# A two-layer graph network on one core: smaller last groups, and a block's inputs loaded a group early

## The chip, the cores and the metric

The kernel runs on one core of a Trainium2 chip. A core has TensorE (PE in the profile; its weight loads are PEld), VectorE (DVE), ScalarE (ACT), GpSimd (POOL) and SyncE (SP), each with its own queue of instructions that it takes in order, and 16 DMA engines. The metric is device time in microseconds (us) for one execution. The kernel before was timed three times: 4756.89, 4762.15 and 4760.23 us, median 4760.23.

## The reference, cut to what matters

There are 12,500 nodes of 128 numbers and 200,000 edges, sorted by destination. An edge's type is the argmax of ten of its 42 attributes. Each layer takes, for every node and type, the mean of the source rows of its edges, multiplies it by the matrix of the type and sums over types; a second matrix (root) is applied to the node's own row.

```python
def _rgcn_layer(x, src, dst, edge_type, w_rel, root, bias):
    N = x.shape[0]
    seg = dst * NUM_REL + edge_type
    xs = x[src]
    sums = jax.ops.segment_sum(xs, seg, num_segments=N * NUM_REL)
    cnt = jax.ops.segment_sum(jnp.ones(seg.shape, x.dtype), seg, num_segments=N * NUM_REL)
    mean = (sums / jnp.maximum(cnt, 1.0)[:, None]).reshape(N, NUM_REL, -1)
    return jnp.einsum('nrd,rdo->no', mean, w_rel) + x @ root + bias
...
edge_type = jnp.argmax(msg[:, NODE_EMB_DIM:-NODE_EMB_DIM], axis=1).astype(jnp.int32)
h = jax.nn.relu(_rgcn_layer(x, src, dst, edge_type, w_rel1, root1, b1))
return _rgcn_layer(h, src, dst, edge_type, w_rel2, root2, b2)
...
x = _layernorm(x + _L0_gnn_ref(...), axis=-1)
```

The second layer gathers rows of `h` from anywhere, so none of its gathers can start before the whole of `h` is written.

## The kernel before

**Tiles and groups.** The edges form 1563 tiles of 128, and the tiles form groups (`groups`, L67): 97 of 16 tiles, then one of 8 and one of 3. For each layer, `layer` (L518) goes over the groups.

**What a group does.** `sums` (L454) issues one gather for each tile on GpSimd (L445; tile `g`, a ring of three groups), lets VectorE build one-hot matrices `oh` (L461; two buffers) and placing matrices `at` (L465), and multiplies `g` by `oh` on TensorE into `zp` (L468): for each tile 12 neighbouring nodes by 10 types. ACT copies `zp` to `zs` (L482; four tiles an instruction). `project` (L487) multiplies `zs` by the ten type matrices, ten matmuls for each half of 8 tiles (L494), and ACT copies the result to `ms` (L500 or L498). `add` (L505) places the rows with `at` (L510) and VectorE adds them to the accumulators of all nodes, `acc` (L516), at an offset that it has loaded from `bt`. `b8` holds the first node of each tile of a group, from which `at` is made.

**Order in the loop.** In the turn of group k, the add of group k-2 is written first, then `sums` of k, then `project` of k-1. In an ordinary group the `zp` matmuls run from the last tile to the first, so that the first of them waits for all gathers of the group. In the last two turns (`end`, L536) they run forward, each after its own gather, and projection and addition of older groups are written earlier. The text is in program order; a scheduler then sets the order of each engine's queue, from the dependencies and its own estimates of time, within what the buffers allow. An engine takes its queue in order.

**Finishing a block.** Nodes are finished in blocks of 512 (23 of them), then of 128 (five) and 84, as soon as all edges that can reach a block are added (`done_after`, L76). `add_oldest` (L527) calls `block_in` (L373) and then `hidden` (layer 1) or `final` (layer 2). `block_in` has SP load the block's rows of x (`xb`; in layer 2 also its rows of h, `hb`; one buffer each), transposes them on TensorE (L386, up to four matmuls) into a PSUM tile `pf` and lets ACT copy that to `fT` (L388). `block_rows` (L391) adds the bias on VectorE (`a`, L395) and multiplies `fT` by the root matrix (L400) and `a` by the identity (L401), by turns, into another `pf`. `hidden` ends with a ReLU (L414) and a store to `hD`; `final` adds `xb` (`v`, L426), normalizes and stores the output. The two `pf` buffers also serve the counting of edges (`count`, L325), which runs beside layer 1 for the next 128 tiles at a time.

Of the kernel before, what the change touches and what calls it, by code (L numbers as in the profile page):

```python
# [20 lines left out]
P = 128  # L21
# [5 lines left out]
G = 16  # L27
QB = 4
HT = 8
# [5 lines left out]
CT = 128  # L35
YB = 512
W = 128
GT = 125
# [5 lines left out]
def rgcn_resnorm_kernel(ctx: ExitStack, tc: tile.TileContext, x, src, dst, attr, w_rel1, root1, b1,  # L44
# [14 lines left out]
    nc = tc.nc  # L59
    N, C = x.shape  # L60
    E = src.shape[0]
    D = attr.shape[1]
    CE = CT * P
    NT = -(-E // P)
    NCH = -(-NT // CT)

    groups = [(t, G) for t in range(0, NT - G + 1, G)]  # L67
    t = NT // G * G
    groups += [(t, HT), (t + HT, NT - t - HT)] if NT - t > HT else [(t, NT - t)]
    NG = len(groups)  # L70
    NPAD = N + SW
    starts = list(range(0, N - YB - 2 * P, YB))
# [1 line left out]
    NBLK = len(starts)  # L74

    def done_after(k):  # L76

        if k == NBLK - 1:
            return NT
        f = starts[k + 1] / N  # L80
        t = int((E * f + 5 * (E * f * (1 - f)) ** 0.5) / P) + 2
        if t >= NT:
            return NT
        return min(a + n for a, n in groups if a + n >= t)

    HALF = NT * P - E
    assert C == P and E % GT == 0 and 0 < HALF < P and NT % CT and groups[-1][1] > 1

    const = ctx.enter_context(tc.tile_pool(name="const", bufs=1))
    dram = ctx.enter_context(tc.tile_pool(name="dram", bufs=1, space=DRAM))  # L90
# [52 lines left out]
    def then(engine, ins):  # L143

        if engine in loaded:
            loaded.remove(engine)
            tc.keep_in_program_order(ins)
        return ins
# [74 lines left out]

    bt = keep.tile([1, NG], I32, name="bt")
    b8_i = keep.tile([G, NG], I32, name="b8_i")
    full = NT // G
    nc.vector.memset(b8_i[:, full:], 0)
    nc.scalar.dma_start(bt[:, :full + 1], bass.AP(dst.tensor, dst.offset, [[1, 1], [G * P, full + 1]]))
    nc.scalar.dma_start(b8_i[:, :full], bass.AP(dst.tensor, dst.offset, [[P, G], [G * P, full]]))
    for k, (t, n) in list(enumerate(groups))[full:]:  # L230
        if k > full:
            nc.scalar.dma_start(bt[:, k:k + 1], bass.AP(dst.tensor, dst.offset + t * P, [[1, 1], [1, 1]]))
        m = n if t + n < NT else n - 1
        nc.scalar.dma_start(b8_i[:m, k:k + 1], bass.AP(dst.tensor, dst.offset + t * P, [[P, m], [1, 1]]))
    nc.scalar.dma_start(b8_i[m:n, NG - 1:], bass.AP(dst.tensor, dst.offset + E - P, [[1, 1], [1, 1]]))
    b8 = keep.tile([G, NG], F32, name="b8")
    place = keep.tile([HR, 2, NG], F32, name="place")
# [119 lines left out]
    def block(k):  # L357
        n0 = starts[k]
        n = (starts + [N])[k + 1] - n0
        return n0, n, [(t, min(P, n - t * P)) for t in range(-(-n // P))]  # L360

    def rows_dma(sb, dr, k, store):
        n0, n, _ = block(k)
        full = n // P
        pairs = []
        if full:
            pairs.append((sb[:, :full], dr[n0:n0 + full * P, :].rearrange("(t p) c -> p t c", p=P)))
        if n % P:
            pairs.append((sb[:n % P, full], dr[n0 + full * P:n0 + n, :]))
        for a, b in pairs:  # L370
            then("SP", nc.sync.dma_start(b, a) if store else nc.sync.dma_start(a, b))

    def block_in(k, l):  # L373

        n0, n, subs = block(k)
        last = "e" if k == NBLK - 1 else ""
        b = len(subs) if last else 4
        xb = fin.tile([P, b, C], F32, name="xb" + last)
        rows_dma(xb, x, k, False)
        fb = xb  # L380
        if l:
            fb = fin.tile([P, b, C], F32, name="hb" + last)
            rows_dma(fb, hD, k, False)
        pt = ps_f.tile([P, YB], F32, name="pf")
        for t, h in subs:
            nc.tensor.transpose(pt[:, t * P:t * P + h], fb[:h, t, :], ident[:h, :h])  # L386
        fT = fin.tile([P, b * P], F32, name="fT" + last)
        nc.scalar.activation(fT[:, :n], pt[:, :n], AF.Copy)  # L388
        return xb, fT
# [53 lines left out]
    def gather(table, t0, n):  # L443
        g = gpool.tile([P, G, C], F32, name="g")
        return g, [then("POOL", nc.gpsimd.indirect_dma_start(  # L445
            out=g[:, j, :], out_offset=None, in_=table, in_offset=bass.IndirectOffsetOnAxis(
                ap=idxE[:, t0 + j:t0 + j + 1], axis=0))) for j in range(n)]
# [3 lines left out]
    def halves(n):  # L451
        return [(h, min(HT, n - h * HT)) for h in range(-(-n // HT))]

    def sums(table, k, end):  # L454

        t0, n = groups[k]
        g, gathers = gather(table, t0, n)
        oh = dpool.tile([P, G, KW], F32, name="oh")
        for j in range(n):
            t = t0 + j  # L460
            then("DVE", nc.vector.tensor_scalar(oh[:, j, :], iotaP[:, :KW], keyE[:, t:t + 1], wE[:, t:t + 1],  # L461
                                                op0=ALU.is_equal, op1=ALU.mult))
        at = spool.tile([HR, 2, SW], F32, name="at")
        for h, _ in halves(n):
            nc.vector.tensor_scalar(at[:, h, :], iotaP[:HR], place[:, h, k:k + 1], None, op0=ALU.is_equal)  # L465
        zp = ps_z.tile([P, G // QB, YB], F32, name="zp")
        for j in range(n) if end else reversed(range(n)):
            m = nc.tensor.matmul(zp[:, j // QB, j % QB * KW:(j % QB + 1) * KW], g[:, j, :], oh[:, j, :],  # L468
                                 start=True, stop=True)
            then("PE", m)  # L470
            if end:
                continue
            if j < n - 1:
                tc.keep_in_program_order(m)
                continue

            for d in gathers[:j]:
                tc.add_manual_dep(m.ins, d.ins.name, whole, reason="one wait per group")
        zs = zpool.tile([P, NREL, G, WN], F32, name="zs")
        for b in range(-(-n // QB)):  # L480
            m = min(QB, n - b * QB)
            then("ACT", nc.scalar.activation(  # L482
                zs[:, :, b * QB:b * QB + m, :],
                zp[:, b, :m * KW].rearrange("c (j r n) -> c r j n", r=NREL, n=WN), AF.Copy))
        return k, zs, at
# [32 lines left out]
    def layer(table, l, finish, steps, flag_too=False):  # L518

        done = 0  # L520
        held, projected = [], []
        ready = flag = None

        def project_oldest():
            projected.append(project(l, *held.pop(0)))

        def add_oldest():  # L527
            nonlocal done
            k, ms, at = projected.pop(0)
            add(k, ms, at)  # L530
            while done < NBLK and sum(groups[k]) >= done_after(done):
                finish(done, ready if done == NBLK - 1 else block_in(done, l))
                done += 1

        for k in range(NG):
            end = k >= NG - 2  # L536
            if projected:
                add_oldest()
            if end:

                if held:
                    project_oldest()
                if not ready:
                    ready = block_in(NBLK - 1, l)
                    if flag_too:
                        loads, (flag,) = nc.values_load_multi_w_load_instructions(
                            flag_i[0:1, 0:1], min_val=0, max_val=1, skip_runtime_bounds_check_because=HELD)
                        for ld in loads:
                            tc.keep_in_program_order(ld)
                        loaded.update(("POOL", "DVE", "PE", "ACT", "SP"))  # L550
            held.append(sums(table, k, end))
            if end and projected:
                add_oldest()
            if len(held) > 1:
                project_oldest()
            if steps:
                till, left, s = steps[0]
                for _ in range(max(1, -(-left[0] // max(1, till - k)))):
                    left[0] -= 1
                    if next(s, steps) is steps:  # L560
                        steps.pop(0)
                        break
        while held or projected:
            if held:
                project_oldest()
            if projected:
                add_oldest()
        return flag
# [13 lines left out]
    for a in range(0, NPAD, YB):  # L582
        m = min(NPAD - a, YB)
# [7 lines left out]
    for c in range(1, NCH):  # L591
        s = [as_steps(sources, c + 1), types(c + 1)] if c + 1 < NCH else []
        todo.append((c * CT // G - 1, [8 + L // DB + 2], chain(*s, count(c))))
    layer(x, 0, hidden, todo)
    def flagged():

# [14 lines left out]
        yield  # L611

    flag = layer(hD, 1, final, [(NG // 2, [1], flagged())], True)
    fast.close()

# [157 lines left out]
```

## Time and profile before

| | |
|---|---|
| median of three runs | 4760.23 us |
| profiled execution, its own time | 4772.34 us |
| its span, first to last instruction | 4770.4 us |
| mean granted TensorE clock | 0.739 |
| PE, PEld busy | 2759.5 us (58%), 2520.6 us (53%) |
| POOL busy | 2955.2 us (62%) |
| DVE, ACT busy | 1511.5 us (32%), 527.0 us (11%) |
| first and last gather of layer 1 start | 4.3 us, 2389.5 us |
| first and last gather of layer 2 start | 2422.2 us, 4731.4 us |

Durations come from the one profiled execution. A row of the timeline has the start (us from the span's start), the duration, engine, line, operation, what is written and read, how many were merged, and in brackets how long the engine was idle before it and what ended that. A row of the groups has the line, engine, operation, names, shape and count, then busy us and mean ns of one, then the idle time just before them and what ended most of it. A row of the waits has the waiting engine and line, what it waited for, us in total, times, and the longest. A row of the windows has the stretch, its length, the busy us (and instructions) of PE, PEld, DVE, ACT and POOL, the granted clock, the DMA engines' busy share and GB/s. "issue" is idle time that ended with nothing that the profile shows; "remote" is a wait whose releaser it does not tell. A matmul in 32-bit floats is two records.

### The profile page before, as it was taken

How to read it: one execution, taken by the hardware profiler on the slowest of the kernel's cores; microseconds unless marked ns; L12 is line 12 of the kernel's file. 1: busy time of each engine (PE TensorE's matmuls, PEld its weight loads, DVE VectorE, ACT ScalarE, POOL GpSimd, SP SyncE). 2: the span in 40 equal slices, each digit the busy share in tenths (PEclk: the TensorE clock that was granted, in tenths of full speed). 3: DMA queues.
4: the chain of work that ended last, by engine and by line, in shares of the span. 5: the costliest groups of instructions: out<-in, count | busy, mean ns of one | idle time of the engine just before them, and what ended most of it. 6: DMA issues, size and time to landing. Idle time of an engine off the chain costs nothing.

```text
span 4770.4 us, 43637 instructions
## 1 busy us (share of the span) xinstructions
PE 2759.5 (58%) x16162; PEld 2520.6 (53%) x16162; DVE 1511.5 (32%) x4652; ACT 527.0 (11%) x1136; POOL 2955.2 (62%) x3142
## 2 busy tenths in 40 slices
PE   2455556555655555666645555666655656565656
PEld 1455555555554545555544555555555555555556
DVE  5233333333333333333222222222222223222323
ACT  1011111111111101111110111111111111111111
POOL 5666665666656666666546666666666666666663
PEclk9677777777777777777776777777777777777778
DMA  4122122122221221212111211221222222222211
GB/s 141 44 79 74 50 74 74 50 75 62 61 77 47 75 62 51 57 48 52 46 49 46 54 52 51 53 56 51 52 56 53 52 52 58 51 52 52 58 52 40
DMA packets 180554, 279.00 MB, mean 58 GB/s; under 512 B 55623, under 2 KB 127190, under 8 KB 177206
## 3 DMA queue, kind: packets, MB, share of 16 engines
q0 software_dynamic: 100032, 205.07, 16.9%
q1 hardware_dynamic: 75428, 69.58, 4.6%
q8 instruction: 132, 2.16, 0.2%
q10 hardware_dynamic: 4872, 1.45, 0.1%
q14 instruction: 90, 0.74, 0.1%
HBM read 262.28 MB, written 13.60 MB: 58 GB/s over the span
## 4 chain that ended last, share of the span: by engine, by line
another core or an unknown queue 34%; PE 33%; issue 21%; DVE 11%; ACT 1%; DMA 0%; DVEq 0%; ACTq 0%; SPq 0%
PE pp L494 16%; PE zp L468 11%; DVE oh L461 7%; PE pp L510 2%; PE pf L401 1%; PE pf L400 1%; DVE at L465 1%; ACT zs L482 1%; DVE acc L516 1%; PE pf L343 0%; PE pf L345 0%; PE pf L386 0%; DVE o L436 0%; DVE st L429 0%
## 5 line engine op out<-in xcount | busy, mean ns | idle before, releaser
L445 POOL DMA_INDIRECT g<-in_x_dram,idxE x1563 | 1475.9, 944 | 911.2 <-issue 445.8
L445 POOL DMA_INDIRECT g<-hD,idxE x1563 | 1476.6, 945 | 865.3 <-issue 455.6
L494 PE MATMUL pp<-w,zs 128*96 128x128 f32 x7840 | 1358.2, 336 | 860.4 <-issue 722.1
L494 PEld LDWEIGHTS pp<-w,zs 128*96 128x96 f32 x7840 | 1232.0, 212 | 982.9 <-issue 834.6
L461 DVE TENSOR_SCALAR oh<-bank,keyE,wE 128x120 f32<-128x120 f32 x3126 | 1000.1, 400 | 644.6 <-remote 576.6
L468 PE MATMUL zp<-oh,g 128*128 128x120 f32 x6252 | 1033.5, 325 | 293.5 <-issue 259.9
L468 PEld LDWEIGHTS zp<-oh,g 128*128 128x128 f32 x6252 | 983.1, 240 | 314.0 <-issue 292.5
L482 ACT ACTIVATE zs<-zp 128x480 f32<-128x480 f32 (+1 forms) x782 | 382.9, 575 | 2167.7 <-remote 1912.9
L516 DVE TENSOR_TENSOR acc<-acc,pp 128x160 f32 x198 | 63.7, 322 | 1634.4 <-remote 1043.0
L510 PE MATMUL pp<-at,ms 96*128 96x160 f32 (+1 forms) x784 | 198.1, 386 | 591.1 <-issue 405.0
L510 PEld LDWEIGHTS pp<-at,ms 96*128 96x128 f32 (+1 forms) x784 | 142.5, 232 | 633.8 <-issue 437.1
L500 ACT ACTIVATE ms<-pp 96x256 f32<-96x256 f32 x196 | 74.1, 378 | 1241.3 <-remote 861.3
L341 DVE TENSOR_TENSOR eqb<-pf,kh 128x1344 bf16<-128x1344 f32 (+1 forms) x65 | 100.6, 1552 | 181.4 <-PE pf L345 82.3
L400 PE MATMUL pf<-root,fT 128*128 128x128 f32 x388 | 110.1, 379 | 79.0 <-issue 49.1
L401 PE MATMUL pf<-ident,a 128*128 128x128 f32 x392 | 114.0, 388 | 60.3 <-DVE a L395 22.0
L400 PEld LDWEIGHTS pf<-root,fT 128*128 128x128 f32 x388 | 87.0, 276 | 91.2 <-issue 55.8
L465 DVE TENSOR_SCALAR at<-bank,place 96x160 f32<-96x160 f32 x392 | 131.9, 376 | 0.0
L401 PEld LDWEIGHTS pf<-ident,a 128*128 128x128 f32 x392 | 90.7, 285 | 68.6 <-issue 24.6
L426 DVE TENSOR_TENSOR v<-pf,xb 128x512 f32<-128x512 f32 (+1 forms) x28 | 17.4, 620 | 243.2 <-remote 238.3
L348 DVE TENSOR_REDUCE wp<-pf 128x128 f32<-128x512 f32 (+1 forms) x13 | 9.0, 691 | 182.9 <-remote 175.5
L343 PE MATMUL pf<-eqb,identb 128*128 128x512 bf16 (+1 forms) x130 | 50.5, 388 | 17.9 <-DVE f L320 17.0
L388 ACT ACTIVATE fT<-pf 128x512 f32<-128x512 f32 (+1 forms) x56 | 30.2, 539 | 207.1 <-remote 151.3
(107 smaller groups left out, 483.0 us busy)
## 6 DMA issues: line engine op xcount, KB each, us to landing
m<-in_edge_attr_dram SPq DMA_DIRECT2D x24, 1344.0 KB
g<-in_x_dram,idxE POOLq DMA_INDIRECT x1563
g<-hD,idxE POOLq DMA_INDIRECT x1563
xb<-in_x_dram SPq DMA_DIRECT2D x46, 256.0 KB
hD<-hb SPq DMA_DIRECT2D x23, 256.0 KB
hb<-hD SPq DMA_DIRECT2D x23, 256.0 KB
out_dram<-o SPq DMA_DIRECT2D x23, 256.0 KB
w<-in_L_gnn_w_rel_dram ACTq DMA_DIRECT2D x2, 640.0 KB
```

Source lines behind the costliest of these rows:

```text
L341: nc.vector.tensor_tensor(eq[:p], kp[:p, None, :R].to_broadcast([p, DB, R]), ahead, op=ALU.is_equal)
L400: nc.tensor.matmul(pr[:h, t, :], fT[:, t * P:t * P + h], rsb[l], start=True, stop=False)
L401: nc.tensor.matmul(pr[:h, t, :], a[:, t * P:t * P + h], ident, start=False, stop=True)
L445: return g, [then("POOL", nc.gpsimd.indirect_dma_start(out=g[:, j, :], out_offset=None, in_=table, in_offset=bass.IndirectOffsetOnAxis(ap= ...
L461: then("DVE", nc.vector.tensor_scalar(oh[:, j, :], iotaP[:, :KW], keyE[:, t:t + 1], wE[:, t:t + 1], op0=ALU.is_equal, op1=ALU.mult))
L465: nc.vector.tensor_scalar(at[:, h, :], iotaP[:HR], place[:, h, k:k + 1], None, op0=ALU.is_equal)
L468: m = nc.tensor.matmul(zp[:, j // QB, j % QB * KW:(j % QB + 1) * KW], g[:, j, :], oh[:, j, :], start=True, stop=True)
L482: then("ACT", nc.scalar.activation(zs[:, :, b * QB:b * QB + m, :], zp[:, b, :m * KW].rearrange("c (j r n) -> c r j n", r=NREL, n=WN), AF.C ...
L494: nc.tensor.matmul(po[:m * WN, h], zs[:, r, h * HT:h * HT + m].rearrange("c j n -> c (j n)"), wsb[l][:, r, :], start=(r == 0), stop=(r == ...
L500: nc.scalar.activation(ms[:, :n // HT], po[:HR, :n // HT], AF.Copy)
L510: nc.tensor.matmul(pa, ms[:m * WN, h], at[:m * WN, h], start=(h == 0), stop=(h == len(parts) - 1))
L516: nc.vector.tensor_tensor(acc[:, s], acc[:, s], pa, op=ALU.add)
```

## The change

The groups are now 95 of 16 tiles, and the last 43 tiles form groups of 8, 8, 8, 8, 4, 4 and 3, so 102 groups in place of 99. `end` holds for these seven. In such a turn the adds and projections of older groups are all written first, `oh` and `at` of the next group (now made by `ones`) are written ahead of the projection, and the group is projected and added in its own turn. The ring stays at three groups. `bt` and `b8_i` are loaded with one pair of DMAs for each size of group: nine in place of six.

`block_in` of the next block to finish is written at the start of the turn after the one that finished the block before (from turn 1 on for the first), in place of right before the finish; the last block is excepted.

```diff
+    NS = NT // G - 2
+    groups = [(t, G) for t in range(0, NS * G, G)]
+    t = NS * G
+    while t < NT:
+        groups.append((t, min(HT if NT - t > 3 * QB else QB, NT - t)))
+        t += groups[-1][1]
...
-    def sums(table, k, end):
+    def ones(k):
         t0, n = groups[k]
-        g, gathers = gather(table, t0, n)
         oh = dpool.tile([P, G, KW], F32, name="oh")
...
+        return oh, at
+
+    def sums(table, k, oh, at):
+
+        t0, n = groups[k]
+        end = k >= NS
+        g, gathers = gather(table, t0, n)
...
             while done < NBLK and sum(groups[k]) >= done_after(done):
-                finish(done, ready if done == NBLK - 1 else block_in(done, l))
+                finish(done, ready if done == NBLK - 1 else given or block_in(done, l))
                 done += 1
+                given = None
         for k in range(NG):
-            end = k >= NG - 2
+            end = k >= NS
+            if k and not given and done < NBLK - 1:
+                given = block_in(done, l)
             if projected:
                 add_oldest()
             if end:
                 if held:
                     project_oldest()
+                    add_oldest()
...
-            held.append(sums(table, k, end))
-            if end and projected:
+            held.append(sums(table, k, *(made or ones(k))))
+            made = ones(k + 1) if end and k < NG - 1 else None
+            if end or len(held) > 1:
+                project_oldest()
+            if end:
                 add_oldest()
-            if len(held) > 1:
-                project_oldest()
```

## The prediction

> **What bounds the kernel now.** GpSimd issues all 3126 gathers, so I read its group on the page first, then its rows in the timeline.
>
> ```profile
> L445 POOL DMA_INDIRECT g<-hD,idxE x1563 | 1476.6, 945 | 865.3 <-issue 455.6
> L494 PE MATMUL pp<-w,zs 128*96 128x128 f32 x7840 | 1358.2, 336 | 860.4 <-issue 722.1
> ```
>
> 945 ns and a pipeline gap of 0.30 us make 1.25 us a gather, 20.0 us for a group of 16. The timeline of layer 2 shows what is added between groups:
>
> ```profile
> 2601.11 0.94 POOL L445 DMA_INDIRECT g<-hD,idxE  x1 [0.30 <-issue]
> 2605.60 0.94 POOL L445 DMA_INDIRECT g<-hD,idxE  x1 [3.54 <-remote]
> ...
> 2628.96 0.94 POOL L445 DMA_INDIRECT g<-hD,idxE  x1 [3.68 <-remote]
> ...
> 2792.63 0.94 POOL L445 DMA_INDIRECT g<-hD,idxE  x1 [3.57 <-remote]
> ...
> 2817.74 0.94 POOL L445 DMA_INDIRECT g<-hD,idxE  x1 [5.37 <-PE zp L468]
> ```
>
> A group's first gather waits for a buffer of the ring of three, so for the `zp` matmuls three groups back. Start to start an ordinary group takes 23.2 us: 20.0 of gathers and a pause of some 3.5 that hardly varies. PE's records cover about 13 of these 23.2, but they run ahead of what other engines see: results come late while gathers are in flight, and the last `zp` of a group is seen about 3.3 us after the last gather. I take the 23.2 as given. What varies is groups in which a block is finished. The 20 such groups in layer 2 from 2792 to 4616 take 24.1 to 25.7, mean 24.87: **1.67 us more** each.
>
> ```profile
> 2798.65 0.60 PE L386 MATMUL pf<-ident,hb 128*128 128x128 f32 x4
> ...
> 2801.95 0.60 ACT L388 ACTIVATE fT<-pf 128x512 f32<-128x512 f32 x1 [1.78 <-PE pp L510]
> ...
> 2805.53 0.32 DVE L516 TENSOR_TENSOR acc<-acc,pp 128x160 f32 x1 [8.39 <-remote]
> ...
> 2806.62 0.80 PE L401 MATMUL pf<-ident,a 128*128 128x128 f32 x2 [2.64 <-DVE acc L516]
> ```
>
> This is one of them. Transposes, their copy and the root matmuls (L400) stand in the same group, in PE's order, and PE stops for the copy. The waits give the sum (us, times, longest):
>
> ```profile
> PEld pf L400 <- ACT fT L388: 35.4, 12, 9.0
> ```
>
> **Block inputs a group early.** SP's loads, four transposes on PE and the copy on ACT move from the finishing group to the group after the previous finish, ahead of that group's add. Their number is unchanged. The trace has a sample: at the start of layer 2 the transposes of its first two blocks run at 2424 to 2429, long before the finishes in the groups that start at 2605.6 and 2698.7. These two groups take 23.4 and 24.3: 0.2 and 1.1 over 23.2, mean 0.65 against 1.67. So I take 1.0 us a finish, 20 finishes: **-20 us** in layer 2. In layer 1, 11 finishing groups with transposes in the same group average 25.3, 2.1 over: 1.45 each, **-16**. Of the others there most share their PSUM buffers with the counting of weights and end in counting groups of 28 to 30 us; I give them nothing. The sum, 36, is as large as the wait row above, though one is not derived from the other. Bounds: at best all the excess of layer 2 goes (24 finishes, 40 us) and the 2.1 of layer 1's eleven (23); at worst nothing.
>
> What the moved work costs: four transposes are 0.6 us of PE records in a group that is held at 23.2 anyway, and PE is then catching up after a finish; 46 times 0.15 = **+7**. Without that cover it is 46 x 0.6 = 28. On ACT the copy (0.60) comes behind `ms` and ahead of the next `zs`, which waits for PE until the group's end; nothing is late. On SP the order is the question: `xb` waits for `v` of the finished block (row at 2815.57, 22.9 into the group; the load goes out at 2816.29). If `hb` goes out behind it, 0.4 later, and lands in the 3.0 us that the load of 2421.32 took until PE's transposes at 2424.29, it is there 27 us after the finishing group's start, 2 into the next. PE gets to the transposes only behind `pp`, some 6 us in. Cover 4 us; if PE met them before, the `add` and all `zp` behind would stand for up to those 4 us.
>
> **The last 43 tiles.** Before, as 16, 16, 8, 3 (layer 1):
>
> ```profile
> 2368.72 0.94 POOL L445 DMA_INDIRECT g<-in_x_dram,idxE  x1 [4.88 <-PE zp L468]
> ...
> 2377.46 0.94 POOL L445 DMA_INDIRECT g<-in_x_dram,idxE  x1 [0.30 <-issue]
> 2387.03 0.94 POOL L445 DMA_INDIRECT g<-in_x_dram,idxE  x1 [8.63 <-PE zp L468]
> ...
> 2422.18 0.94 POOL L445 DMA_INDIRECT g<-hD,idxE  x1 [31.70 <-DMA hD<-hb]
> ```
>
> From 2321.0: 23.2 + 24.5 + 18.3 (8 tiles: 10 of gathers, 8.3 pause) + 3.5 + 31.7 = **101.2 us**. The 31.7 is a drain, and PE works in it:
>
> ```profile
> 2368.70:2387.00 18.30, 13.33 (x84) 13.14 (x84) 6.28 (x22) 2.83 (x8) 7.55 (x8) 0.74 0.20 51
> 2387.00:2422.20 35.20, 30.63 (x254) 28.33 (x252) 16.43 (x85) 9.29 (x26) 2.86 (x4) 1.00 0.11 30
> ```
>
> 30.6 of 35.2 us busy, at the full granted clock (1.00). So small groups remove little PE work: 7 groups need 70 `pp` matmuls where four need 60, one costs 0.21 us there, plus three adds: +3 us. And the ring holds three *groups*: smaller ones mean fewer tiles ahead. Step by step, each from one gather start to the next, PE bound (full speed: 16 `zp` 3.4, 20 `pp` 4.4, add and copies 1.5; 8 tiles: `zp` 1.7, wait for `zs` 1.2, `pp` 2.1, `ms` and add 1.1):
> - first 8: `pp`, add, 16 `zp` with 5 us lost beside 8 gathers, 15.5; second 8, with a block of 512, 19. Before, 23.2 and 24.5: -13.2.
> - third 8: two `pp` of 16, two adds with blocks, 8 `zp`: 21. Fourth 8: wait, `pp`, add, block, 8 `zp` with a loss: 12.
> - 4, 4: 7 each. The last 3: from its first gather, three groups of `zs`, `pp`, `ms`, add at some 5 (before, the 8 and the 3 took 4.7 and 5), the last block, store: 24.
>
> Sum 105.5, **+4 us a layer**. Bounds from the same rows: four groups of 8 at 13.3 (10 of gathers and the 3.3), two of 4 at 8.3 and 20 at the end give 90, -11; 18.3 for each 8, 10 for each 4 and 30 at the end, as before, give 123, +22. The sum lies between, and I keep it, since its steps are those of the rows just shown.
>
> **A rule against the row.** The Trainium skill, "TensorE: Matmul & The Clock Gate", section "HAM oscillation", says that PE's clock falls to half only after idle stretches of over about 3.4 us. My waits for `zs` are 1.2 us, so by the rule the end groups keep full speed. But the row of the one 8-tile group says 0.74: beside its gathers PE started nothing from 2374.9 to 2379.9, longer than its own waits would make it. By the rule my sum stays 105.5; by the row, for the fourth 8 and both 4s (3.8 us of `zp` and `pp` each: 11.4/0.74 - 11.4 = 4), it is 109.5. I take the row for the 8 alone, +1, and the rule for the 4s, whose 5 us of gathers are too short for such a stand: 106.5, **+5 a layer, +10 in all**.
>
> At the start three more small loads go out on ACT's queue (0.26 to 0.7 us each), ahead of the first activation at 16.3; the first `zp` is at 86. Nothing.
>
> **Sum**: -20 - 16 + 7 + 10 = **-19 us**. The profiled execution took 4772.34 (span 4770.4), 12 above the runs' median, so I take the 19 from the median 4760.23: **4741 us**.
>
> **Rivals.**
> 1. Both parts gain: early inputs give the 36 at no cost and the end 11 a layer: -58, 4702. For it: the drains, 32 and 38 us, are the largest single idle times of GpSimd. Against: PE is busy in them.
> 2. The small groups lose the prefetch: every group of 8 pays the pause of 8.3, every 4 one of 5: +22 a layer, -29 elsewhere: +15, 4775, slower. It decides once the seven groups take over 116 us (101.2 and half of the 29). For it: the 8.63 above. Against: that group had a whole 16 of `zp` behind it.
> 3. Transposes stand for `hb`: 4 us x 23 finishes in layer 2, +92 +10 and no gain, 4862. Against: the 4 us of cover.
> 4. The order on PE stays as it was, because the scheduler, not the program's text, places the transposes: only +10, 4770.
>
> **Chances**: forecast 0.42 (own range 4720 to 4756), rivals 0.20, 0.17, 0.08, 0.13. The range to hold 8 in 10 reaches to half of rival 1 and past rival 2: 4700 to 4786. With 0.2% (9.5 us) as what a measurement tells from no change: faster 0.53, same 0.16, slower 0.31.
>
> **What would show it.** Finishing groups of layer 2 at about 23.9 instead of 24.9, and the wait of L400 for `fT` near nothing; ordinary groups still 23.2. From the first gather of tile 1520 to layer 2's first gather 106, drain from the last gather below 25 instead of 31.7. It is wrong if ordinary groups grow, if transposes wait for DMA, or if the pauses after groups of 8 pass 8 us.

## Result and profile after

| | before | after |
|---|---|---|
| median, six runs each | 4757.30 us (4754.01 to 4762.15) | 4710.64 us (4699.18 to 4727.02) |
| profiled execution, its own time | 4772.34 us | 4727.02 us |
| its span | 4770.4 us | 4725.1 us |

The changed kernel takes 0.9908 of the time before (95% interval 0.9894 to 0.9922): 46.7 us less between the medians, 45.3 us between the two profiled spans. By the 0.2% that the prediction set as a limit that is faster, as forecast. It is inside the range to hold 8 in 10 (4700 to 4786), but the gain is more than twice the 19 us of the sum, outside the forecast's own range (4720 to 4756), and nearer to rival 1 (4702) than to the forecast (4741).

The spans are split at the first gathers of five stages. The first gather of tile 1520 starts the last 43 tiles.

| stage | before | after | difference | predicted |
|---|---|---|---|---|
| start, to the fourth group of layer 1 | 92.7 | 94.1 | +1.4 | 0 |
| layer 1, from there to tile 1520 | 2228.3 | 2200.7 | -27.6 | -16 + 3.5 |
| layer 1, last 43 tiles to layer 2's first gather | 101.2 | 98.2 | -3.0 | +5 |
| layer 2, to tile 1520 | 2240.5 | 2224.5 | -16.0 | -20 + 3.5 |
| layer 2, last 43 tiles to the end | 107.7 | 107.6 | -0.2 | +5 |

(The 7 us for moved transposes are shared out evenly.) Layer 2 came as worked out. Layer 1 gave twice as much, and the tails nothing worth the name. On the page of the changed kernel the rows of the gathers and of the projection are (busy us, mean ns, idle before):

```profile
L450 POOL DMA_INDIRECT g<-hD,idxE x1563 | 1476.8, 945 | 849.0 <-issue 452.7
L505 PE MATMUL pp<-w,zs 128*96 128x128 f32 x7880 | 1330.2, 333 | 675.3 <-issue 544.7
```

Neither engine works faster; both stand less. The timeline of layer 2 shows a finishing group and the group behind it:

```profile
2763.92 0.94 POOL L450 DMA_INDIRECT g<-hD,idxE  x1 [3.49 <-remote]
...
2769.49 0.39 PE L405 MATMUL pf<-root,fT 128*128 128x128 f32 x2
...
2777.85 0.80 PE L406 MATMUL pf<-ident,a 128*128 128x128 f32 x2 [3.98 <-DVE acc L527]
...
2787.49 0.94 POOL L450 DMA_INDIRECT g<-hD,idxE  x1 [3.88 <-PE zp L479]
...
2792.66 0.60 PE L391 MATMUL pf<-ident,hb 128*128 128x128 f32 x4
...
2803.16 0.38 ACT L511 ACTIVATE ms<-pp 96x256 f32<-96x256 f32 x1 [12.83 <-remote]
...
2803.59 1.44 PE L521 MATMUL pp<-at,ms 96*128 96x160 f32 x4 [10.32 <-issue]
...
2808.78 0.36 SPq L376 DMA_DIRECT2D hb<-hD  x1
2808.79 0.60 ACT L393 ACTIVATE fT<-pf 128x512 f32<-128x512 f32 x1 [5.25 <-remote]
...
2811.35 0.94 POOL L450 DMA_INDIRECT g<-hD,idxE  x1 [4.21 <-PE zp L479]
```

The finishing group (2763.92 to 2787.49, 23.6 us) begins its root matmuls with an `fT` that was made groups ago. The transposes of the next block (2792.66) stand one group later, and that group takes 23.9. Over the 22 finishing groups of layer 2 ahead of tile 1520 the mean is 23.71 (before 24.78); the groups behind them take 23.75 (before 23.36). The copy to `fT` comes at 2808.79, 15.5 us after the end of the transposes, and now nothing waits for it. ACT had the copy `ms` to do first, and that too starts 10.3 us after the end of its matmuls (2792.83); then ACT stands another 5.25 us. At the same moment SP's load goes out into the `hb` that the transposes read (2808.78, SPq). So two engines see PE's result that late. Whether the matmuls end later than they are drawn, or the news of it travels late, these rows don't tell.

The tail of layer 1, GpSimd's first gathers of its groups and of layer 2:

```profile
2306.74 0.94 POOL L450 DMA_INDIRECT g<-in_x_dram,idxE  x1 [2.29 <-PE zp L479]
...
2324.88 0.94 POOL L450 DMA_INDIRECT g<-in_x_dram,idxE  x1 [8.47 <-PE zp L479]
...
2344.65 0.94 POOL L450 DMA_INDIRECT g<-in_x_dram,idxE  x1 [10.08 <-PE zp L479]
...
2393.00 0.94 POOL L450 DMA_INDIRECT g<-hD,idxE  x1 [18.56 <-issue]
```

The drain fell from 31.7 to 18.6 us, and the pauses ahead of it took most of that back: 8.5 and 10.1 where there had been 4.9 and 8.6, and the last four groups start later by their own small pauses.

### The profile page after: what moved, and what is told of

The parts are those of the page before. It is cut to its first block, busy times and chain, and to the rows that moved or that the text cites. A ratio compares the mean times of both kernels' runs of the same rounds, so it can differ in the third digit from the quotient of the medians.

```text
span 4725.1 us, 43784 instructions
## 1 busy us (share of the span) xinstructions
PE 2749.6 (58%) x16206; PEld 2523.4 (53%) x16206; DVE 1509.7 (32%) x4660; ACT 529.7 (11%) x1142; POOL 2955.3 (63%) x3142
## 4 chain that ended last, share of the span: by engine, by line
another core or an unknown queue 37%; PE 29%; issue 18%; DVE 14%; ACT 1%; DMA 0%; DVEq 0%; ACTq 0%; SPq 0%
PE pp L505 13%; PE zp L479 10%; DVE oh L465 9%; PE pp L521 2%; PE pf L406 1%; PE pf L405 1%; DVE at L469 1%; DVE acc L527 1%; ACT zs L493 1%; PE pf L350 0%; PE pf L348 0%; PE pf L391 0%; DVE st L434 0%; DVE bank L275 0%
## 5 line engine op out<-in xcount | busy, mean ns | idle before, releaser
L505 PE MATMUL pp<-w,zs 128*96 128x128 f32 x7880 | 1330.2, 333 | 675.3 <-issue 544.7
L505 PEld LDWEIGHTS pp<-w,zs 128*96 128x96 f32 x7880 | 1218.7, 210 | 787.8 <-issue 649.8
L521 PE MATMUL pp<-at,ms 96*128 96x160 f32 (+1 forms) x788 | 206.5, 396 | 682.5 <-issue 498.5
L511 ACT ACTIVATE ms<-pp 96x256 f32<-96x256 f32 (+1 forms) x198 | 74.2, 375 | 1321.1 <-remote 1010.0
```

The costliest lines, as they stand in the source:

```text
L505: nc.tensor.matmul(po[:m * WN, h], zs[:, r, h * HT:h * HT + m].rearrange("c j n -> c (j n)"), wsb[l][:, r, :], start=(r == 0), stop=(r == ...
L511: nc.scalar.activation(ms[:, :n // HT], po[:HR, :n // HT], AF.Copy)
L521: nc.tensor.matmul(pa, ms[:m * WN, h], at[:m * WN, h], start=(h == 0), stop=(h == len(parts) - 1))
```

## Experiments

All ran beside the kernel before on the same chip, but on three chips: here A, B and C. The kernel before takes 3973 us on A, 4680 to 4686 us on B and C, against 4757 us in the first measurement ("the first chip" below). What follows is always a comparison on one chip.

Two things are followed throughout. One is the row of PE's weight loads for the root matmuls, with the time for which PE stood idle ahead of them. The other, matched block by block in the trace, is the lag from the end of a block's transposes to the start of the copy `fT`, over the 23 blocks of 512 in layer 1.

**1. One part alone (chip A).** The early inputs alone are this edit of the kernel before:

```diff
-                finish(done, ready if done == NBLK - 1 else block_in(done, l))
+                finish(done, ready if done == NBLK - 1 else given or block_in(done, l))
                 done += 1
+                given = None
...
+            if k and not given and done < NBLK - 1:
+                given = block_in(done, l)
```

> The kernel before with one part of the change: a block's inputs are loaded and transposed a group early; groups as before (97 of 16, 8, 3). Theory A, the early inputs are the gain: about 43 us below the kernel before (ratio 0.991), layer 2 from its first gather to that of tile 1520 about 16 us shorter, layer 1's some 28, and both tails as before (101 and 108 us). Theory B, the small last groups give a good part of it: at most 25 us below the kernel before.

The small groups alone are the rest of the change (`groups`, `bt`, `ones`, the order under `end`), with `block_in` left at the finish.

> The other part alone: the small last groups and their order in the loop, a block's inputs loaded where they are finished. Theory A: 0 to 4 us below the kernel before, tails of 98 and 107 us. Theory B: 15 us or more below. The recorded sum had this part at 10 us above.

Loads alone: `block_in` is cut in two, and only its loads go out early.

```diff
+            if k and not given and done < NBLK - 1:
+                given = block_in(done, l)
...
-        pt = ps_f.tile([P, YB], F32, name="pf")
+        return xb, fb
+
+    def turned(k, given):
...
+        pt = ps_f.tile([P, YB], F32, name="pf")
...
-                finish(done, ready if done == NBLK - 1 else block_in(done, l))
+                finish(done, ready if done == NBLK - 1 else turned(done, given or block_in(done, l)))
```

> The kernel before, with the loads of xb and hb alone written a group early; transposes, their copy and PE's queue stay as before. Theory A, PE's order is what counts (transposes, copy and root matmuls no longer in one group): within 5 us of the kernel before. Theory C, what the finish waited for was the loads: about 40 us below.

Transposes three times, where they stand before:

```diff
-        for t, h in subs:
+        for t, h in 3 * subs:
             nc.tensor.transpose(pt[:, t * P:t * P + h], fb[:h, t, :], ident[:h, :h])
```

> The kernel before, with every transpose of a block written three times where it is finished: 8 more a finish, 1.2 us of PE. Theory A, PE is late in a finishing group and pays for each instruction there: finishing groups of layer 2 grow by about 1.2 us, the whole by 45 to 55 us. Theory D, only the wait for ACT's copy counted: below 10 us.

Measured: kernel before 3972.95; early inputs 3972.90 (ratio 1.0000, 0.9991 to 1.0009); groups 3960.34 (0.9968, 0.9956 to 0.9980); loads 3973.74 (1.0002); three times 3973.40 (1.0000). Theory A's numbers failed in three of the four. Theory B's 15 us for the groups was missed too, by 2.4; theory D's number held. The run with the loads can't tell the theories apart here, since there was nothing to gain. The page of the run with early inputs says why:

```profile
L445 POOL DMA_INDIRECT g<-hD,idxE x1563 | 1475.3, 944 | 496.3 <-issue 462.0
...
L494 PE MATMUL pp<-w,zs 128*96 128x128 f32 x7840 | 892.9, 273 | 6.4 <-ACT zs L482 3.3
```

A gather still takes 944 ns, but GpSimd's idle time is 496 us in place of 865: nearly all of it the 0.30 us between two gathers. Ordinary groups take 20.0 us, with no pause. The projection's matmuls take 273 ns with 6.4 us of idle time, where the first chip showed 336 ns and 860 us in the kernel before. PE is ahead of the gathers, so nothing that it does in a finishing group is on the path, 8 more transposes included. The copy follows the transposes at once:

```profile
2785.35 0.60 PE L386 MATMUL pf<-ident,hb 128*128 128x128 f32 x4
...
2785.99 0.60 ACT L388 ACTIVATE fT<-pf 128x512 f32<-128x512 f32 x1
```

What is left on this chip is the drain between the layers, here with the groups of before and then with the small ones:

```profile
1992.70 0.94 POOL L445 DMA_INDIRECT g<-hD,idxE  x1 [20.26 <-DMA hD<-hb]
```

```profile
1983.64 0.94 POOL L450 DMA_INDIRECT g<-hD,idxE  x1 [12.07 <-issue]
```

8.2 us less, and from the last gather to the end 27.3 against 23.2: together 12.3, nearly the whole 12.6 of the measurement. Where PE isn't late the prediction's two parts change places.

**2. The changed kernel, and PE made late by force (chip B).** First the changed kernel as it is:

> The changed kernel itself, on the chip of this call. Where the kernel before takes some 3973 us here and GpSimd's gathers never pause (period of an ordinary group 20.0): all of the gain is that of the small last groups, 12 to 13 us below the kernel before. Where the kernel before takes some 4757 us (period 23.2): 40 to 48 us below, as first measured.

4634.64 against 4685.97, ratio 0.9896 (0.9881 to 0.9911): 51 us, a little above the 40 to 48. Its ordinary groups take 23.0 us: this chip resembles the first. Then the projection four times, without and with early inputs:

```diff
-            for r in range(NREL):
+            for r in 4 * list(range(NREL)):
                 nc.tensor.matmul(po[:m * WN, h], zs[:, r, h * HT:h * HT + m].rearrange("c j n -> c (j n)"),
                                  wsb[l][:, r, :], start=(r == 0), stop=(r == NREL - 1))
```

> The kernel before with every matmul of the projection run four times (each repeat starts its sum anew, so the result stays), some 13 us more of PE a group, so that PE is late wherever it runs. Theory A: ordinary groups grow to 23 us or more, finishing groups are longer still by 2 to 4 us; 4500 us or more in all. It is the base for the run that follows.

> The kernel above (projection four times) with a block's inputs loaded and transposed a group early, groups as before. Theory A, where PE is late it stops for the copy fT in a finishing group, and an early block takes that stop away: 0.5 to 1.5 us a finish for 46 finishes, 20 to 70 us below the kernel with the fourfold projection. Theory E, PE only carries the same instructions in another place and what was gained came from something else: within 5 us of it.

7406.44 and 7409.75 us: no gain (ratios 1.5808 and 1.5824, intervals of 0.0021 to either side). Theory A fails in the form given, "where PE is late it stops for the copy". PE is late here: an ordinary group takes 36.8 us, 13.8 over 23.0, which is 0.23 for each of its 60 added matmuls. Yet it hardly stops. In the first of the two the groups of instructions show 2.6 us of idle time (behind the bar) ahead of all root matmuls:

```profile
L400 PEld LDWEIGHTS pf<-root,fT 128*128 128x128 f32 x388 | 59.2, 192 | 2.6 <-ACT fT L388 2.5
```

The lag from transposes to copy is 0.04 us in all 23 blocks. In these groups the gathers stop 17 us before the group ends. Theory E's number (within 5 us) held, but with no stop to take away this pair can't speak for it; part 4 can. So PE being late isn't the condition; it is that its result is *seen* late, which on this chip went with gathers in flight, though not every time (part 4).

**3. The root matmuls early too (chip B).** In layer 2 the root matmuls of `fT` run in `block_in`, and `block_rows` adds only `a`:

```diff
+        if not l or k == NBLK - 1:
+            return xb, fT
+        pr = ps_f.tile([P, 4, C], F32, name="pf")
+        for t, h in subs:
+            nc.tensor.matmul(pr[:h, t, :], fT[:, t * P:t * P + h], rsb[l], start=(t == 0), stop=False)
+        return xb, pr
...
+        if l and k < NBLK - 1:
...
+            for t, h in subs:
+                nc.tensor.matmul(fT[:h, t, :], a[:, t * P:t * P + h], ident, start=False, stop=(t == len(subs) - 1))
+            return fT
```

> The changed kernel, in whose second layer the root matmuls of fT also run a group early, their sums held open in PSUM until those of a close them. Where PE is late (23.2 us a group): 5 to 15 us below the changed kernel, since the finishing groups' rest of 0.45 us over an ordinary one is PE work too. Where gathers never pause: within 3 us of the changed kernel.

4649.64 us: 15.0 *above* the changed kernel (ratio to before 0.9925 against 0.9896). Layer 2 as far as tile 1520 is 12.7 us longer; 10.3 of that is left when the one odd group of each kernel is taken out (9.5 and 6.7 us over the median, with no cause in the profile). Finishing groups are down to 23.08 (medians; 23.14 in the changed kernel), but the groups behind them take 23.67 in place of 23.07. There transposes and root matmuls stand in one group again:

```profile
3006.26 0.60 PE L391 MATMUL pf<-ident,hb 128*128 128x128 f32 x4
...
3013.01 0.60 ACT L393 ACTIVATE fT<-pf 128x512 f32<-128x512 f32 x1 [3.87 <-remote]
...
3013.66 2.08 PE L398 MATMUL pf<-root,fT 128*128 128x128 f32 x8 [2.72 <-issue]
...
3025.06 0.94 POOL L461 DMA_INDIRECT g<-hD,idxE  x1 [4.48 <-PE zp L490]
```

The copy starts 6.2 us after the transposes' end, PE stands until 3013.66, 0.05 us after the copy's end, and the next group's gathers start after a pause of 4.48 instead of 3.3. The groups of instructions have 49.8 us of idle time ahead of layer 2's root matmuls, where the changed kernel has 2.4:

```profile
L398 PEld LDWEIGHTS pf<-root,fT 128*128 128x128 f32 x194 | 41.5, 313 | 49.8 <-issue 26.6 <-ACT fT L393 23.2
```

So it isn't an early place that helps. A group *between* the transposes and the first reader of `fT` does, and this kernel took it away again.

**4. One part alone once more (chip B).** The edits of part 1.

> The early inputs alone once more (groups as before), for a chip on which PE is late. Where the kernel before takes some 4690 to 4760 us: theory A, the early inputs are nearly all of the gain, 35 to 50 us below the kernel before, finishing groups of layer 2 within 0.6 us of ordinary ones; theory B, the small last groups share it: 15 to 30 us below. Where it takes some 3973 us: no difference again.

> The small last groups alone once more. Where the kernel before takes some 4690 to 4760 us: theory A, within 8 us of the kernel before; theory B, 15 to 30 us below; the recorded sum, 10 us above. Where it takes some 3973 us: 12 to 13 us below again.

> The loads alone a group early, transposes, copy and PE's queue as before, once more. Where the kernel before takes some 4690 to 4760 us: theory A (PE's stop for the copy fT inside the finishing group was the cost), within 8 us of the kernel before; theory C (the loads were late), the same gain as with the transposes moved too. Where it takes some 3973 us: no difference again.

| chip B | median us | ratio (interval) | lag in layer 1: median, longest |
|---|---|---|---|
| before | 4684.03 | | |
| early inputs alone | 4636.21 | 0.9894 (0.9879 to 0.9909) | 3.10, 8.91 |
| small groups alone | 4684.56 | 0.9995 (0.9986 to 1.0005) | 2.91, 13.55 |
| loads alone | 4687.82 | 1.0004 (0.9995 to 1.0013) | 2.25, 13.12 |

Theory A holds here on all three counts, and B and C fall. All of the 48 us is that of the early inputs; loads without transposes bring none of it, groups bring none. The medians hide a split. With small groups or loads alone, ten of the 23 lags, all in groups with counting, are 10.6 to 13.6 us; their transposes end 9 to 13 us after the group's first gather. With early inputs the transposes stand elsewhere, and ten lags are 0.04 us: six with transposes in the first 3.6 us of a group, beside its gathers, and four behind a group's last gather. The other lags are 2.5 to 8.9 us, and PE no longer stands for them. The groups of instructions of the root's weight loads, with early inputs, with small groups, with loads alone:

```profile
L400 PEld LDWEIGHTS pf<-root,fT 128*128 128x128 f32 x388 | 69.7, 220 | 43.8 <-issue 39.8 <-DVE eqb L341 3.1 <-ACT fT L388 0.7
```

```profile
L405 PEld LDWEIGHTS pf<-root,fT 128*128 128x128 f32 x388 | 82.6, 263 | 137.5 <-ACT fT L393 77.5 <-issue 59.8
```

```profile
L408 PEld LDWEIGHTS pf<-root,fT 128*128 128x128 f32 x388 | 80.2, 255 | 136.0 <-ACT fT L396 80.4 <-issue 55.5
```

Not every "issue" is free of the copy: with loads alone, the first root matmul starts within 0.2 us of the end of its copy in 44 of the 46 blocks of 512. Counted by these starts, 134.7 of the 136.0 us are stops for the copy; with early inputs 1.1 of the 43.8 are. The stop is gone, but PE's standing mostly moved: ahead of the matmuls of `a` it rose from 28.8 to 110.1 us, so the two rows together lost 11 us while the kernel lost 48. What the change is worth can't be read from idle time; the lengths of the groups, below, tell it.

The two runs also show the wait at work. With loads alone, a finishing block in layer 1 beside the counting of edges:

```profile
719.58 0.66 PE L394 MATMUL pf<-ident,xb 128*128 128x128 f32 x4
...
724.76 0.51 PE L502 MATMUL pp<-w,zs 128*96 128x128 f32 x1 [1.14 <-issue]
...
731.96 0.38 SPq L371 DMA_DIRECT2D xb<-in_x_dram  x1
731.96 0.60 ACT L396 ACTIVATE fT<-pf 128x512 f32<-128x512 f32 x1 [17.06 <-remote]
...
732.27 0.94 POOL L453 DMA_INDIRECT g<-in_x_dram,idxE  x1 [3.43 <-remote]
...
732.61 0.80 PE L408 MATMUL pf<-root,fT 128*128 128x128 f32 x2 [7.34 <-ACT fT L396]
```

The transposes end at 720.24. ACT is idle (17.06 us) and starts the copy only at 731.96, when the group's gathers have stopped; SP's next load into `xb` goes out in the same moment. PE stands 7.34 us for the copy. The counting comes behind, and the next group takes 27.9 us. With early inputs, in the groups of the same tiles:

```profile
725.24 0.90 PE L386 MATMUL pf<-ident,xb 128*128 128x128 f32 x4
...
726.17 0.60 ACT L388 ACTIVATE fT<-pf 128x512 f32<-128x512 f32 x1 [0.99 <-PE pf L386]
```

By then the block before has its root matmuls behind it, these transposes belong to the next one, and the group takes 23.7.

Where it goes, from the traces of these two runs on one chip, each layer from its fourth group to tile 1520: layer 1, 2178.2 to 2144.3 (-33.9); layer 2, 2139.5 to 2130.3 (-9.2); the tails -3.5 and -3.8. In layer 1 the excess over the median group (23.04 and 23.06) fell from 35.6 to 12.0 us in the 36 groups with counting, and from 18.8 to 6.0 in the 12 finishing groups without it. In the groups with counting, two things changed at once: PE's stop went, and the blocks' two `pf` buffers, which the counting shares, are taken at another time. No run separates these.

**5. A deeper ring (chip C).** The changed kernel with `RING = 4` for `RING = 3`.

> The changed kernel with four group buffers for the gathered rows in place of three. It asks what holds an ordinary group at 23.2 us. Theory A, PE's rate beside gathers does, and a gather's pause only passes that on: where the kernel before takes 4690 to 4760 us, ordinary groups stay at 23 us and the whole within 10 us of the changed kernel (ratio to the kernel before 0.988 to 0.992). Theory F, the gathers wait only because the ring is short: the pauses of 3 us go, some 190 of them, 500 us or more below. Where the kernel before takes some 3973 us there are no pauses, and it equals the changed kernel (ratio 0.997).

4640.85 against 4679.65, ratio 0.9918 (0.9903 to 0.9932): not better than three buffers (0.9896 on chip B). Theory A holds. Two first gathers in layer 2:

```profile
2497.24 0.95 POOL L450 DMA_INDIRECT g<-hD,idxE  x1 [3.27 <-remote]
...
2520.27 0.95 POOL L450 DMA_INDIRECT g<-hD,idxE  x1 [3.32 <-remote]
```

The first pause comes a group later than with three buffers (after the fourth group of a layer), and then the period is 23.0 again. On chip B no run beat the changed kernel by more than the intervals leave open; on chip A it was not run.

## Why the prediction was right, and where not

**Early inputs, layer 2: right.** "So I take 1.0 us a finish": 1.07 (24.78 to 23.71). So close a hit is partly luck, since the sample was two groups, 0.2 and 1.1 us over. The moved work, put at 0.15 a group, cost 0.39 in the group behind (23.36 to 23.75) on the first chip and nothing on chip B. The net, -16.0, is within a microsecond of the -16.5; on chip B it was -9.2.

**Early inputs, layer 1: the mis-sized term.** "Of the others there most share their PSUM buffers with the counting of weights [...]; I give them nothing." On the first chip the excess over the median group (23.24 us before, 23.23 after) fell by 17.1 us (58.2 to 41.1) in the 36 groups with counting, on chip B by 23.6. That is the step that failed: a term put at nothing was worth the most, and even the bound "at best" for layer 1 (23) was passed by the 27.6. The finishing groups without counting gave 8.2 on the first chip (27.6 to 19.4), less than the 16, because one of them grew to 29.9; the other ten that had been long fell by 13.3. The block at 719.58 above is one of those with counting: there the lag is long, and so is the stop.

The warning was in the profile of before. The 35.4 us of waits for `fT` were set beside the sum of both layers ("as large as the wait row above") without asking where they lie. Here are the waits of these loads in layer 1, then those in layer 2 (us in total, times, longest):

```profile
PEld pf L400 <- ACT fT L388: 34.7, 11, 9.0
PEld pf L400 <- issue: 25.1, 13, 8.4
```

```profile
PEld pf L400 <- issue: 31.0, 22, 2.3
...
PEld pf L400 <- ACT fT L388: 0.7, 1, 0.7
```

The named wait is one of layer 1, all but 0.7 us, with single stops of up to 9.0 us; that this total agreed with the sum was chance. Layer 2 has the same stop under another name. Of its 22 entries of "issue", 1.4 us each, one is drawn in the prediction's own rows: the copy of 2801.95 ends at 2802.55, and the first root matmul starts at 2802.60. So it starts in 45 of the 46 blocks of 512, 0.05 us behind the copy's end but for one at 0.43. In the changed kernel that row of layer 2 is 1.1 us, and in layer 1 no root matmul starts within 0.2 us of its copy's end. Here too the standing moved: ahead of the matmuls of `a` from 20.6 to 93.5 us in layer 1 and from 47.8 to 89.4 in layer 2, and in layer 1 the root's loads still have 52.7 us (59.8 before), none of it a stop for the copy. So the "wait of L400 for `fT` near nothing" came true, and was no measure of the gain.

**SP's order, rival 3: right to be put low.** The cover of 4 us was not used up. PE's transposes wait for `hb` 7.4 us in all in the changed kernel, 6.8 before, 4.7 to 4.9 of it in a single wait.

**The tails: wrong, "+5 a layer".** Measured -3.0 and -0.2; the small groups alone -0.05% on chip B. The steps of layer 1, predicted and measured: 15.5 and 12.0; 19 and 18.1; 21 and 19.8; 13 and 11.8; 7 and 8.4; 7 and 6.2; 24 and 22.0. Two terms carry 5.5 of the 8.3 us: the "5 us lost" in the first group of 8, 3.5 of which did not come, and the last step with the drain. Other sizes of group were not tried. The pauses after groups of 8 pass 8 us, one of the signs named against the forecast, and the time fell all the same: what they cost the drain gave back. Rival 2 (116 us) is out. Rival 1 came nearest by its total, and its first half held (early inputs at no net cost, 43.6 us for its 36); its 11 a layer at the end came nowhere. Nearest is chip A, with 8.2 and 4.1.

**The rule against the row: neither came out.** The windows of the changed kernel for the fourth 8 and both 4s of layer 1 (stretch, length, busy PE, PEld, DVE, ACT, POOL, granted clock, DMA share, GB/s):

```profile
2344.70:2356.50 11.80, 7.01 (x49) 6.11 (x46) 3.62 (x13) 2.07 (x8) 7.53 (x9) 0.84 0.24 66
2356.50:2364.90 8.40, 7.83 (x41) 7.34 (x41) 3.23 (x11) 1.56 (x5) 3.82 (x5) 0.61 0.25 71
2364.90:2371.10 6.20, 5.12 (x41) 4.71 (x41) 2.40 (x10) 1.36 (x5) 3.78 (x5) 1.00 0.15 42
```

For the 8 I took the clock of the row (0.74) and got 0.84; for the 4s I took the rule's full speed and got 0.61 and 1.00. The clock falls inside the first two of these stretches: it is 0.50 from 2352.8 to 2362.9. PE's longest stand from 2325 to there was 2.93 us, shorter than the rule asks, so the rule as I used it doesn't give this fall. The first 4 is the one step of the tail that came out longer than predicted, by 1.4 us.

**"I take the 23.2 as given": half right.** The sums held with it. But "a group that is held at 23.2 anyway" claimed slack for PE, and the fourfold projection shows that there is none of any size (13.8 us more for 60 matmuls), while a fourth buffer shows that the ring isn't what holds it. Both point to PE's pace beside gathers; why PE's instructions stand there ("issue", 722 us of the projection before) stays open. One part of it was in the profile of before and was not followed. PE's waits ahead of the adding matmuls (L510):

```profile
PE pp L510 <- issue: 405.0, 134, 12.0
...
PE pp L510 <- ACT ms L500: 184.2, 23, 20.8
```

This is the same hand-over, and nearly every group has it: PE projects, ACT copies to `ms`, PE reads it. Of 591.1 us ahead of these matmuls, 590.9 end within 0.2 us of the end of a copy `ms`, "issue" or not. The changed kernel has 682.5, chip B 397.6 (loads alone), chip A 7.3 (early inputs). No run moved this hand-over, so what it costs is not shown.

**Rival 4 (the order on PE stays) fell:** the profile after has the transposes where the text puts them.

## What to carry to other kernels

Split a wait's row by stage before setting it beside a sum; two totals that agree say nothing about where either lies. Where one engine hands a result to a second and needs the answer back, put a whole stretch of work between the hand-over and the reader: moving the pair together, however early, only moves the stop. And a gain that comes from lateness goes where the lateness goes: on a chip whose PE kept up, the early inputs were worth nothing and the small groups 0.3%.

## What the runs showed of the hardware

**One kernel, three paces.** The same program took 4757, 4680 to 4686, and 3973 us, with gathers of 944 to 949 ns on all. What sets chip A apart is PE beside gathers: no "issue" idle time in the projection there, 722 us on the first chip, 948 on chip B (loads alone); ordinary groups of 20.0, 23.2 and 23.0 us. Between the first chip and B that row goes the other way than the time. The mean granted clock of the kernel before differs far less (0.768 to 0.772 on A, 0.739 on the first, 0.742 to 0.754 on B). No run tells the cause.

**PE's results seen late.** From the end of a block's transposes to the copy that waits for them: 0.04 us (median, layer 1) on chip A, 2.25 on chip B (loads alone) and up to 13.1. It is 0.04 on chip B too once the gathers stop early in the group (fourfold projection), and with early inputs in six blocks whose transposes stand in the first 3.6 us of a group. The ten lags of over 10 us with loads alone belong to transposes that end 9.7 to 13.1 us into their group. The releaser of such a wait often reads "remote" in the profile, and the matmul that it waits for has long been drawn as done.
